# Emptying a PSUM bank with one relu copy, adding beta to x ahead, and scaling means on ScalarE, in a four-layer graph attention stack

## The chip, the cores and the metric

The kernel runs on one core of a Trainium2 chip. The metric is the device time of one execution in microseconds. The engines are TensorE (PE in the profile; its weight loads are PEld), VectorE (DVE), ScalarE (ACT), GpSimd (POOL) and SyncE (SP), which only issues DMAs. Each engine works through its own queue in order; semaphores order the engines among themselves.

## The reference

There are 16 graphs of 1024 nodes with 256 features, and four layers. Each layer adds to `x` what an attention over the graph's edges makes of the normalised, relu'd `x`. The third layer is the one that the change touches most:

```
h = maximum(layernorm(x), 0)                       # every layer, over the 256 features
v = h @ W                                          # layers 0 to 2: four heads of 64; layer 3: one of 256
e = leaky_relu(s_src[i] + s_dst[j]); e = -inf where adj[i, j] == 0
out = softmax(e over j) @ v
x = x + out                                        # layers 0, 1 and 3
# layer 2, the third one, per head:
o = relu(softmax(e) @ v + bias) + v
x = x + (o - mean(o)) / sqrt(var(o) + 1e-6) * gamma + beta
```

## The kernel before

**What is on the chip.** Nodes are tiled by 128: a graph has 8 blocks (`NB`). `x_cur` holds a graph's `x` in SBUF through all layers (128 x 8 x 256, float32); it is changed in place. A *unit* is one layer of one graph. For a head `h` of a unit, the numerators of the softmax are made transposed, block `j` of the sources against all 1024 targets: `cover` is one VectorE instruction (`SCALAR_TENSOR_TENSOR p<-r,fac,mask`, 128x1024) that writes one of 12 tiles `p`. Its operand `r` is a PSUM tile with a row spread over the partitions, which ScalarE copies there (`COPY r<-rows`).

**Groups and banks.** `gather` multiplies a tile `p` by the 64 columns of `v` and a column of ones. Eight tiles (`j` = 0 to 7) add up in one PSUM bank, called `po`: one bank for one half (`i`, four blocks of 128 targets) of one head, of 4 x 65 columns. This is a *group*. There are two `po` banks, so a group can only begin when the group before the last has left its bank. All matrix products are in float32. In the third layer the columns come from `v_flat`, a copy of `v` with the bias added.

**Emptying a bank.** `evacuate` (line 1312) does it. In the first two layers ScalarE copies the whole bank to the SBUF tile `att` (`COPY att<-po`, 128x260), and the division by the sums is done later in `finish`. In the third layer VectorE first takes the reciprocal of the four sums in the bank (line 1325), and then ScalarE takes each of the four blocks through a relu with the reciprocal as its scale, from the bank to `att` (lines 1327 and 1328). The bank is free when the last of the four is done. There are 16 x 4 x 2 = 128 such evacuations. There are three `att` tiles (`ATTS`); one is in use from the first evacuation of a head to the end of its `finish`.

**Finishing a head.** In the third layer `finish` (line 1341) adds `v` to `att` (128x512), VectorE makes statistics (`bn_stats`, eight of 128x64), GpSimd merges them (`merged`, with a power for the inverse root), ScalarE normalises with eight instructions (`ACTIVATE att<-att,s`), and then come three 128x512 instructions: times gamma, plus beta (line 1384), and the add to `x_cur` (line 1385). `either` gives these to GpSimd, or to VectorE at the very end of the kernel. When all heads of a unit are finished, the next layer of that graph may be prepared.

**Preparing a unit.** `prepare` (line 949) makes the statistics of `x_cur`, normalises (`hn`), transposes on TensorE, takes the relu on ScalarE (`hT<-pp`) and projects (`pp<-wa,hT`), and ScalarE copies the result to `v` (`v<-pp`, `v_one<-pp` for the last layer). Two banks, `pp`, serve these and the last layer's sums. For the first layer of the graphs from the third on (`ACT_STATS`, `BY_ACT`), 14 units, ScalarE makes the statistics: eight sums, then GpSimd scales them by -1/256 (line 974), then eight sums of squares about that mean.

**Order.** The order on every engine is made while the program is built. `Plan` keeps a clock for each engine and a table of costs; the loop at line 1589 always takes the step that can begin first, among jobs written as generators (`yield engine, ready`). An engine wrapped by `plan.engine` books its cost with each instruction; `nc.scalar`, `nc.vector` and `nc.gpsimd` issue without booking, and `plan.spend` books without issuing. The order of three graphs in different layers is interleaved (`ORDER`), so that the last layer's sums, the projections and the groups of several graphs share TensorE. The wrapper is the reason why nearly every line of the profile carries line 515.

Of the kernel before, what the change touches and what calls it, by code (L numbers as in the profile page):

```python
# [16 lines left out]
AF = mybir.ActivationFunctionType  # L17
ALU = mybir.AluOpType
# [518 lines left out]
def fast_path(  # L537
# [21 lines left out]
    nc = tc.nc  # L559
    ctx.enter_context(tc.manual_schedule())  # L560
    plan = Plan()
    pe, act, dve, pool, sp = (
        plan.engine(e, name)
        for e, name in (
            (nc.tensor, "PE"),
            (nc.scalar, "ACT"),
            (nc.vector, "DVE"),
            (nc.gpsimd, "POOL"),
            (nc.sync, "SP"),
        )  # L570
    )
    G, N, F = x.shape
# [3 lines left out]
    QUAD = 4  # L576
# [31 lines left out]
    bias_r, gamma_r, beta_r = (const.tile([P, F], F32, name=n) for n in ("bias_r", "gamma_r", "beta_r"))  # L608
# [46 lines left out]
    def bank():  # L655
        k = min(free_banks(), key=lambda k: banks[k])
        banks[k] = None
        if k >= BANKS:
            spare[0] += 1
            return ps_o.tile([P, 512], F32, name="po"), k  # L660
        return ps_p.tile([P, 512], F32, name=f"pp{k}"), k
# [20 lines left out]
    def wide_bank(dt=F32):  # L682
        k = wide_free.index(min(t for t in wide_free if t is not None))
        wide_free[k] = None
        return ps_r.tile([P, 4096 // mybir.dt.size(dt)], dt, name=f"r{k}"), k
# [249 lines left out]
    def merged(st: bass.AP, rs: bass.AP, w: int, eps: float, eng=pool):  # L935

        m0, m1, q0, q1 = st[:, :, 0, 1], st[:, :, 1, 1], st[:, :, 0, 2], st[:, :, 1, 2]
        shift, spread, inv = (rs[:, i, :] for i in range(3))
        eng.tensor_tensor(inv, m0, m1, ALU.subtract)
        eng.tensor_tensor(spread, q0, q1, ALU.add)  # L940
        eng.tensor_tensor(inv, inv, inv, ALU.mult)
        eng.tensor_tensor(shift, m0, m1, ALU.add)
        eng.tensor_scalar(inv, inv, 0.25, eps, ALU.mult, ALU.add)
        eng.tensor_scalar(spread, spread, 1.0 / w, 0.0, ALU.mult, ALU.add)
        eng.tensor_tensor(spread, spread, inv, ALU.add)
        pool.tensor_tensor(inv, spread, neg_half, ALU.pow)
        eng.tensor_scalar(shift, shift, -0.5, 0.0, ALU.mult, ALU.add)

    def prepare(u: "Unit"):

        n, w, layer = u.n, u.w, u.layer
# [16 lines left out]
        st = small.tile([P, NB, 2, 3], F32, name="st", bufs=2)  # L968
        rs = small.tile([P, 3, NB], F32, name="rs", bufs=4)
        if by_act:  # L970
            for i in range(2 * NB):
                if i == NB:
                    yield "POOL", None
                    pool.tensor_scalar(rs[:, 0, :], st[:, :, 0, 0], -1.0 / F, 0.0, ALU.mult, ALU.add)
                if i:
                    yield "ACT", None
                seen = work.tile([P, N], FP8, name="seen", bufs=1)[:, : 2 * F].bitcast(BF16)
                b, c = i % NB, i // NB
                if c:
                    act.activation(  # L980
                        seen, xt[:, b, :], AF.Square, bias=rs[:, 0, b : b + 1], accum_out=st[:, b, 1, 0:1]
                    )
                else:
                    act.activation(seen, xt[:, b, :], AF.Identity, accum_out=st[:, b, 0, 0:1])
            yield "POOL", None
            pool.tensor_scalar(rs[:, 1, :], st[:, :, 1, 0], 1.0 / F, 1e-5, ALU.mult, ALU.add)
            pool.tensor_tensor(rs[:, 2, :], rs[:, 1, :], neg_half, ALU.pow)
        else:
            for i in range(NB):
                if i:  # L990
                    yield "DVE", None
                dve.bn_stats(st[:, i].rearrange("p c s -> p (c s)"), xt[:, i, :])
            eng, name = (dve, "DVE") if u is main[0] else either()
            yield name, None
            merged(st, rs, F, 1e-5, eng)
            u.g.centred = plan.now
# [26 lines left out]
        if u is main[0]:  # L1023
            keep_warm(WARM_MAX)
        yield "PE", free_bank
        pm, k = bank()
# [10 lines left out]
            scale=top,  # L1037
# [4 lines left out]
        pa, k = bank()  # L1042
# [9 lines left out]
        eng, name = (dve, "DVE") if u is main[0] else either()  # L1052
# [29 lines left out]
        if direct:  # L1082
# [5 lines left out]
            for h in range(DIRECT_HEADS if n > 1 else 1):  # L1088
                pr, k = wide_bank()
# [22 lines left out]
        pr, k = bank()  # L1112
        turned(pr, mine[:, 0, :])
        yield "DVE", None, AT_ONCE
        row = small.tile([P, P // 2], F32, name="row", bufs=1)
# [196 lines left out]
    def evacuate(u: "Unit", i: int, h: int, po, turn: int):  # L1312

        w = u.w
        q = slice(i * QUAD, (i + 1) * QUAD)
        yield "ACT" if u.shared else "DVE", lambda: finishing[0] < ATTS or (u, h) in taking
        if (u, h) not in taking:
            finishing[0] += 1
            taking[u, h] = [work.tile([P, NB, w + 1], F32, name="att", bufs=ATTS), 0]
        att = taking[u, h][0]  # L1320
        if u.shared:
            act.copy(att[:, q, :], po)
        else:
            inv = u.inv[:, h, q]
            dve.reciprocal(inv, po[:, :, w])
            yield "ACT", None
            for k in range(QUAD):
                act.activation(att[:, i * QUAD + k, :w], po[:, k, :w], AF.Relu, scale=inv[:, k : k + 1])
        opened[turn] = plan.now
        taking[u, h][1] += 1  # L1330
        if taking[u, h][1] == 2:

            by = -(10**6) if u.layer < 2 or at_tile[0] > len(tiles) - LAST else at_tile[0] + LATER
            add(by, finish(u, h, att[:, :, :w], att[:, :, w]), plan.now)

    def either():

        idle = at_tile[0] == len(tiles) and plan.free["DVE"] <= plan.free["POOL"] + SOONER
        return (dve, "DVE") if idle else (pool, "POOL")

    def finish(u: "Unit", h: int, att, total):

        n, w = u.n, u.w
        at = h * (w + 2)
        wide = lambda ap: ap.unsqueeze(2).to_broadcast([P, NB, w])
        row = lambda ap: ap[:, h * w : (h + 1) * w].unsqueeze(1).to_broadcast([P, NB, w])
        xs = u.g.x[:, :, h * w : (h + 1) * w]

        eng, name = either()
        if u.shared:  # L1350
            yield "DVE", None
            dve.reciprocal(u.inv[:, h, :], total)
            eng, name = either()
            yield name, None
            eng.tensor_mul(att, att, wide(u.inv[:, h, :]))
        else:
            yield name, None
        if u.layer == 2:
            eng.tensor_add(att, att, u.v[:, :, at : at + w])
            u.added += 1  # L1360
            u.v_done = u.added == n
            yield "DVE", None
            s = small.tile([P, 4, NB], F32, name="s", bufs=ATTS)
            st = small.tile([P, NB, 2, 3], F32, name="st64", bufs=ATTS)
            for b in range(NB):
                dve.bn_stats(st[:, b].rearrange("p c s -> p (c s)"), att[:, b, :])
            eng, name = either()
            yield name, None
            merged(st, s, w, 1e-6, eng)
            if name == "DVE":  # L1370
                yield "DVE", None
                eng.tensor_add(att, att, wide(s[:, 0, :]))
                eng.tensor_mul(att, att, wide(s[:, 2, :]))
            else:
                pool.tensor_mul(s[:, 1, :], s[:, 0, :], s[:, 2, :])
                for b in range(NB):
                    yield "ACT", None
                    act.activation(
                        att[:, b, :], att[:, b, :], AF.Identity, bias=s[:, 1, b : b + 1], scale=s[:, 2, b : b + 1]
                    )  # L1380
                eng, name = either()
                yield name, None
            eng.tensor_mul(att, att, row(gamma_r))
            eng.tensor_add(att, att, row(beta_r))
        eng.tensor_add(xs, att, xs)
        finishing[0] -= 1
        u.finished[h] = plan.now
        if len(u.finished) == n:
            u.spent = True
            yield "DVE", None  # L1390
            at = u.g.b * LAYERS + u.layer
            inv = u.inv.rearrange("p h b -> p (h b)")
            dve.tensor_reduce(greatest[:, at : at + 1], inv, AX.X, ALU.add)
            summed.append(plan.now)
# [189 lines left out]
    def add(until, gen, ready, first=None):  # L1584
        jobs.append([until, ready, *(first or next(gen))[:2], gen])
# [103 lines left out]
```

## Time and profile before

| | |
|---|---|
| median of 3 runs | 2668.16 us (2663.21 to 2668.47) |
| profiled execution | 2667.53 us, span of its instructions 2665.8 us |
| granted TensorE clock | 0.997 |
| TensorE busy | 2578.2 us, 97% |
| VectorE busy | 2342.0 us, 88% |
| GpSimd busy | 1890.4 us, 71% |
| ScalarE busy | 1272.3 us, 48% |
| DMA | 69 GB/s on average, 184.44 MB |

In a line of a group, `out<-in` are the program's tiles with buffer numbers left out, then the shapes, the number of instructions, the busy time in us and the mean duration in ns, and behind the bar the idle time of the engine before them and what ended it. In a timeline, a line begins with the start in us and the busy time in us; lines that follow each other on one engine are merged; in square brackets stands the idle time before and what ended it. In the waits, "A <- B: total, times, longest" is time for which A's engine was idle until B was done. "issue" is a wait for nothing that the profile shows. The busy time of a matmul is modelled from its start, so that TensorE can be shown as busy for some tens of ns in which it waits.

### The profile page before, as it was taken

The page shows a single profiled execution, that of the slowest core. Times are in us where ns is not written, and L with a number is a line of the kernel's source. Part 1 is how long each engine was busy: PE and PEld are TensorE (multiplying, and loading weights), DVE is VectorE, ACT ScalarE, POOL GpSimd, SP SyncE. Part 2 cuts the span into 40 slices and gives each one's busy share as a digit, 9 for nine tenths or more (in the row PEclk, how much of TensorE's full clock was granted, in tenths as well). Part 3 has the DMA queues.
Part 4 walks back from the last instruction along what each step waited for, and adds up shares of the span by engine and source line. Part 5 has one row for each costly group of instructions (what it writes and reads, how often), then busy time and mean ns, then how long its engine had stood idle before and what let it go on. Part 6 is the DMA issues. An engine that isn't in the chain of part 4 may idle for free. (4 is left out here: it accounts for less than half of the span.)

```text
span 2665.8 us, 132436 instructions
## 1 busy us (share of the span) xinstructions
PE 2578.2 (97%) x59354; PEld 2207.9 (83%) x59354; DVE 2342.0 (88%) x3723; ACT 1272.3 (48%) x3378; POOL 1890.4 (71%) x3375
## 2 busy tenths in 40 slices
PE   9999999999999999999999999999999999899998
PEld 7888887787988788889888788988778798888775
DVE  6799998897999797889998897999888699998984
ACT  4633563654346456533564644356364553443441
POOL 5556888765778877747887875688787565977761
PEclk9999999999999999999999999999999999999999
DMA  8533233443132253313314441323334441111100
GB/s 133 84 75 73 59 69 69 76 87 71 64 66 63 63 85 82 76 57 77 72 55 82 88 72 59 83 50 75 74 74 79 83 85 57 53 47 55 40 23 32
DMA packets 211122, 184.44 MB, mean 69 GB/s; under 512 B 150640, under 2 KB 184560, under 8 KB 210544
## 3 DMA queue, kind: packets, MB, share of 16 engines
q1 hardware_dynamic: 143088, 159.10, 20.7%
q0 software_dynamic: 67456, 16.78, 10.3%
q8 instruction: 467, 7.65, 1.2%
q14 instruction: 111, 0.91, 0.1%
HBM read 191.77 MB, written 34.39 MB: 85 GB/s over the span
## 5 line engine op out<-in xcount | busy, mean ns | idle before, releaser
L515 DVE SCALAR_TENSOR_TENSOR p<-r,fac,mask 128x1024 f32<-128x1024 f32 (+2 forms) x2032 | 2075.7, 1079 | 159.8 <-PE pp L515 80.8
L515 PE MATMUL po<-v,p 128*64 128x65 f32 x32992 | 1060.9, 224 | 36.4 <-issue 15.8
L515 PEld LDWEIGHTS po<-v,p 128*64 128x64 f32 x32992 | 1021.5, 138 | 87.9 <-issue 30.8
L515 PEld LDWEIGHTS po<-v_flat,p 128*64 128x64 f32 x16384 | 507.8, 138 | 56.8 <-issue 24.4
L515 PE MATMUL po<-v_flat,p 128*64 128x65 f32 x16384 | 525.0, 223 | 29.4 <-issue 14.7
L515 PE MATMUL pp<-wa,hT 128*64 128x264 f32 (+1 forms) x4032 | 474.2, 385 | 0.1
L515 PE MATMUL pp<-v_one,p 128*64 128x257 f32 x3584 | 403.6, 380 | 3.2 <-ACT y L515 2.9
L515 PEld LDWEIGHTS pp<-wa,hT 128*64 128x64 f32 x4032 | 278.4, 137 | 132.1 <-ACT v L515 0.4
L515 PEld LDWEIGHTS pp<-v_one,p 128*64 128x64 f32 x3584 | 248.6, 136 | 128.0 <-ACT y L515 4.6
L515 POOL TENSOR_SCALAR hn<-x_cur,rs 128x256 f32<-128x256 f32 x504 | 274.6, 558 | 33.3 <-PE pp L515 29.3
L515 POOL TENSOR_TENSOR att<-att,inv 128x512 f32<-128x512 f32 x128 | 133.7, 1045 | 221.2 <-DVE inv L515 207.7
L515 ACT COPY att<-po 128x260 f32<-128x260 f32 x256 | 96.2, 376 | 377.1 <-PE po L515 353.1
L515 ACT COPY v<-pp 128x264 f32<-128x264 f32 (+1 forms) x392 | 148.5, 379 | 215.0 <-PE pp L515 213.8
L515 POOL TENSOR_TENSOR x_cur<-att,x_cur 128x512 f32<-128x512 f32 x190 | 225.8, 1188 | 14.9
L515 ACT COPY r<-rows 128x1024 f32<-128x1024 f32 x190 | 194.0, 1021 | 21.8 <-DVE p L515 15.5
L515 ACT ACTIVATE att<-att,s 128x64 f32<-128x64 f32 x512 | 190.9, 439 | 23.3 <-POOL s L515 23.0
L515 ACT ACTIVATE hT<-pp 128x512 f32<-128x512 f32 x250 | 136.4, 598 | 128.1 <-PE pp L515 127.4
L515 ACT ACTIVATE att<-po,inv 128x64 f32<-128x64 f32 x512 | 118.7, 321 | 145.6 <-DVE inv L515 143.6
L515 POOL TENSOR_TENSOR y<-y,x_cur 128x256 f32<-128x256 f32 x116 | 84.3, 732 | 131.6 <-ACT y L515 112.1
L515 POOL TENSOR_TENSOR v<-v,fac 128x512 f32<-128x512 f32 x131 | 136.2, 1064 | 11.5 <-ACT fac L515 11.4
L515 DVE BATCH_NORM_STATS2 st<-x_cur 128x6 f32<-128x256 f32 x400 | 138.3, 411 | 3.3 <-DMA x_cur<-in_x_dram 2.9
L515 PE MATMUL pp<-ident,hn 128*128 128x128 f32 x1000 | 137.0, 280 | 0.2 <-DVE row L515 0.2
(124 smaller groups left out, 2150.0 us busy)
## 6 DMA issues: line engine op xcount, KB each, us to landing
rows<-line SPq DMA_DIRECT2D x190, 512.0 KB
out_dram<-y SPq DMA_DIRECT2D x128, 128.0 KB
x_cur<-in_x_dram SPq DMA_DIRECT2D x112, 128.0 KB
near<-in_adj_dram POOLq DMA_DIRECT2D x112, 128.0 KB, 4.3
rows_one<-line SPq DMA_DIRECT2D x13, 512.0 KB
x_cur<-in_x_dram SPq DMA_DIRECT2D x4, 512.0 KB
line<-row SPq DMA_DIRECT2D x96, 8.0 KB
block<-in_adj_dram POOLq DMA_DIRECT2D x4, 256.0 KB, 10.4
```

The lines of the kernel that those rows point to most:

```text
L515: r = call(*a, **k)
```

## The change

In `evacuate`, for the third layer: ScalarE copies the whole bank through a relu to `att`, VectorE takes the reciprocals of the sums from `att`, and ScalarE multiplies the four blocks in `att`, in place. In `finish`, for the third layer: beta is added to `x_cur` right behind the add of `v` to `att`, on the same engine; the add of beta to `att` is gone. In `prepare`: the 128x8 means are scaled by ScalarE. The new instructions are issued without booking, and what they replace is booked where it was.

```
@@ prepare @@
                 if i == NB:
                     yield "POOL", None
-                    pool.tensor_scalar(rs[:, 0, :], st[:, :, 0, 0], -1.0 / F, 0.0, ALU.mult, ALU.add)
+                    nc.scalar.activation(rs[:, 0, :], st[:, :, 0, 0], AF.Copy, scale=-1.0 / F)
+                    plan.spend(
+                        "POOL", *plan.cost("POOL", "tensor_scalar", (rs[:, 0, :],), {}), [st.tensor.name], [rs.tensor.name]
+                    )
@@ evacuate @@
             inv = u.inv[:, h, q]
-            dve.reciprocal(inv, po[:, :, w])
+            nc.scalar.activation(att[:, q, :], po, AF.Relu)
+            nc.vector.reciprocal(inv, att[:, q, w])
+            plan.spend("DVE", *plan.cost("DVE", "reciprocal", (inv,), {}))
             yield "ACT", None
             for k in range(QUAD):
-                act.activation(att[:, i * QUAD + k, :w], po[:, k, :w], AF.Relu, scale=inv[:, k : k + 1])
+                one, of = att[:, i * QUAD + k, :w], inv[:, k : k + 1]
+                nc.scalar.activation(one, one, AF.Copy, scale=of)
+                plan.spend("ACT", *plan.cost("ACT", "activation", (one, of), {}), [], [att.tensor.name])
@@ finish @@
             eng.tensor_add(att, att, u.v[:, :, at : at + w])
+            {"DVE": nc.vector, "POOL": nc.gpsimd}[name].tensor_add(xs, xs, row(beta_r))
...
             eng.tensor_mul(att, att, row(gamma_r))
-            eng.tensor_add(att, att, row(beta_r))
+            plan.spend(name, *plan.cost(name, "tensor_add", (att,), {}), [att.tensor.name], [att.tensor.name])
         eng.tensor_add(xs, att, xs)
```

## Prediction

> **What bounds the kernel now.** I read the page first, then who waits for whom on TensorE, then the busy time of each engine in stretches of the span.
>
> ```profile
> span 2665.8 us, 132436 instructions
> PE 2578.2 (97%) x59354; PEld 2207.9 (83%) x59354; DVE 2342.0 (88%) x3723; ACT 1272.3 (48%) x3378; POOL 1890.4 (71%) x3375
> ```
>
> TensorE is the bound over the whole span: it is idle for 2665.8 - 2578.2 = 87.6 us, and no change to the other engines can give back more. The waits split that idle time:
>
> ```profile
> PE po L515 <- ACT att L515: 15.8, 16, 1.4
> PE po L515 <- DVE p L515: 9.4, 9, 2.7
> ```
>
> The first line is what the relu copy aims at: a group's PSUM bank (`po`) was not yet emptied. I followed each of these waits in the timeline: 13, of 11.5 us in all, stand before the first matmul of a group whose bank a third-layer group held; the longest (1.36 us) recurs at 783.6, 1271.6 and 1756.9 us, so the schedule repeats every 488 us or so. Where do they lie? Stretches of the windows view, one in each repetition (columns: stretch, its length, busy PE, PEld, DVE, ACT, POOL):
>
> ```profile
> 264.00:342.00 78.00, 73.03 (x2136) 67.74 (x2132) 77.75 (x118) 42.01 (x127) 68.06 (x115) 1.00 0.29 60
> 752.00:830.00 78.00, 72.69 (x2115) 67.29 (x2112) 76.89 (x117) 41.38 (x126) 66.68 (x113) 1.00 0.29 59
> 1240.00:1318.00 78.00, 73.13 (x2136) 67.77 (x2134) 77.94 (x118) 41.76 (x128) 67.42 (x113) 1.00 0.30 60
> 1725.00:1803.00 78.00, 73.39 (x2149) 68.06 (x2145) 78.00 (x118) 41.89 (x127) 67.25 (x114) 1.00 0.30 60
> 2255.00:2340.00 85.00, 77.39 (x2183) 72.64 (x2180) 84.60 (x137) 34.07 (x99) 73.98 (x137) 0.96 0.15 49
> ```
>
> Here VectorE is busy 395.2 of 397 us: it, not TensorE, sets the pace. TensorE is idle 27.4 us here, and the timeline shows it taking tile after tile 0.05 us after VectorE made it. Twelve of the 13 bank waits lie in these five stretches; the thirteenth is 0.26 us. Outside them TensorE is the bound and VectorE is some 2 to 8 us of tiles ahead.
>
> **Prices.** From the groups, shapes kept apart:
>
> ```profile
> L515 ACT ACTIVATE att<-po,inv 128x64 f32<-128x64 f32 x512 | 118.7, 321 | 145.6 <-DVE inv L515 143.6 <-DVE wide L515 0.8
> L515 ACT COPY att<-po 128x260 f32<-128x260 f32 x256 | 96.2, 376 | 377.1 <-PE po L515 353.1 <-POOL hn L515 11.3 <-POOL x_cur L515 9.9
> L515 DVE RECIPROCAL inv<-po 128x4 f32<-128x4 f32 x128 | 22.5, 176 | 21.4 <-PE po L515 20.3
> L515 POOL TENSOR_TENSOR att<-att,beta_r 128x512 f32<-128x512 f32 x62 | 73.6, 1187 | 4.9
> ```
>
> The built programs, set side by side, have the same order on TensorE and SyncE; on the others only the changed instructions differ. So every gain or loss is a wait that gets shorter or longer.
>
> **The relu copy.** It adds 128 instructions at 0.376 us (the first two layers' copy of the same 128x260) to ScalarE: 48 us on an engine that is idle half the time, which by itself costs nothing. Three effects matter.
>
> (a) The bank. Before, it was free a reciprocal and four scalings after the group's end: 1.2 to 2.2 us. After, 0.05 + 0.38 = 0.43 us if ScalarE is free. But 11.3 of the 11.5 us lie where VectorE is saturated: TensorE gets its bank earlier and then waits as much longer for the next tile. I take -0.3 us. The bounds are 0 and -11.5.
>
> (b) The reciprocal. It is in VectorE's queue, with the covers (`p`) behind it, and waited for TensorE; now it waits for ScalarE's copy, which ends 0.47 us after the group's end at the earliest. Where VectorE arrived sooner it now stands still. Example, ScalarE's and VectorE's timelines around the group that ended at 294.77:
>
> ```profile
> 294.69 0.93 ACT L515 ACTIVATE att<-po,inv 128x64 f32<-128x64 f32 x4 [0.78 <-DVE inv L515]
> 295.49 1.04 ACT L515 COPY r<-rows 128x1024 f32<-128x1024 f32 x1
> 296.43 0.95 ACT L515 ACTIVATE att<-po,inv 128x64 f32<-128x64 f32 x4
> ...
> 295.74 0.17 DVE L515 RECIPROCAL inv<-po 128x4 f32<-128x4 f32 x1
> ```
>
> In the new order this group's relu stands on ScalarE where the second four scalings stood, behind the first four and the `r` copy: it ends at 296.43 + 0.45 = 296.9, and the reciprocal of 295.74 is 1.2 us late. In the first stretch VectorE loses 0.2 (271.7) + 0.4 (280.3) + 1.2 (295.7), less the 0.25 for which it waited anyway at 308.25: 1.55. In the second 0.4 (758.4) + 0.4 (768.2) + 1.1 (783.7, the same pattern) less 0.15: 1.75; the third the same; the fourth without the first 0.4: 1.4; the fifth 0.4 + 0.5 + 0.4 less 0.15: 1.15. VectorE has no idle time to absorb it there, so the kernel is later by the sum: 7.6 us. Bounds: 2 (one wait of 0.4 in each stretch) and 11 (every wait in them). Outside these stretches VectorE loses some 40 us in the same way, covered by its tiles ahead; with that cover gone it would all count.
>
> (c) What stands behind on ScalarE. Relu, then a trip to VectorE, then the scalings, and ScalarE's next copies wait. ScalarE's timeline from 358 (between the lines shown stand four scalings at 358.86, two `hT` copies at 359.64 and an `r` copy at 360.60):
>
> ```profile
> 357.80 1.06 ACT L515 ACTIVATE seen<-mask 128x1024 fp8e4<-128x1024 fp8e4 x1
> ...
> 361.54 0.97 ACT L515 ACTIVATE att<-po,inv 128x64 f32<-128x64 f32 x4
> 362.33 0.82 ACT L515 COPY v_one<-pp 128x258 f32<-128x258 f32 x2
> ```
>
> Each of the two evacuations grows by about 0.35 (relu) + 0.3 (ScalarE idle during the reciprocal of 0.18 and two signals). The `v_one` copy is then 1.3 us late; TensorE refills its bank at 363.02, 0.3 us after it was free, so TensorE stalls about 1.0 us. This recurs at 846, 1334 and 1819: 4.0 us. Lesser cases of the same kind (505, 992, 1479 and 1965 us: 0.3 each; 2355: 0.3) make 1.5. Around 2510 a late reciprocal and `r` copy delay a tile that TensorE took 0.05 us after it was made: 0.5. Together 6.0; bounds 0 (ScalarE's queue closes up) and 9.
>
> The scalings now read SBUF. The nearest rows are copies scaled by a pointer from SBUF, 299 ns for 128x4 and 309 for 128x16: at that slope 64 elements take 349 ns, against 321 from PSUM. That is 0.03 us each, inside the bounds of (c).
>
> The Trainium skill (Perfetto Trace Analysis, Optimizing Scalar/DVE Operations) speaks against this edit: ScalarE pays about 93 ns of access on SBUF and 51 on PSUM. By it the 512 scalings would cost ScalarE 21 us instead of the 14 that my slope makes. The same page (Optimization Strategy) says that the same gap repeating on the engine that should be saturated can mean too little PSUM for the next tile, which would credit (a) with its full 11.5 us. The stretches above say that another engine is saturated just there.
>
> **Beta ahead.** The number of adds stays. The one behind gamma goes: a head's end comes 1.25 us sooner on GpSimd. The new add follows `att + v` on the same engine, where GpSimd often waits for the statistics (2.3 us at 396). It pays where somebody waits for `x_cur` (the beta add stands just before the first line, at 408.31):
>
> ```profile
> 409.58 1.18 POOL L515 TENSOR_TENSOR x_cur<-att,x_cur 128x512 f32<-128x512 f32 x1
> 410.80 0.38 ACT L515 COPY att<-po 128x260 f32<-128x260 f32 x1 [2.48 <-POOL x_cur L515]
> ```
>
> That copy waits for an `att` buffer, and TensorE is idle 1.25 us for its bank (411.2; also 900.2, 1387.4, 1872.4). The chain gains 1.25 and loses 0.4 to the late reciprocal at 395.7: -0.85 x 4 = -3.4. At the end, VectorE's beta add of 1.25 us at 2597.8 lies on the chain to the last graph's first transpose, before which TensorE is idle 1.83 us: -1.25 + 0.4 = -0.85. Sum -4.3; bounds -6.5 and 0.
>
> **Means by ScalarE.** Fourteen tiny instructions leave GpSimd (204 ns each), with a trip of about 1 us at 330.2, 818.1, 1305.9 and 1791.2. No one on TensorE or VectorE waits for it: 0, bounds -1 and +1.
>
> **Sum.** -0.3 + 7.6 + 6.0 - 4.3 = +9.0 us on the profiled execution's 2667.5 us (span 2665.8 and 1.7 around it): 2676.5. The median of the runs, 2668.2, is 0.6 us above that execution.
>
> **Rivals.**
> - *Faster: the banks pay.* If VectorE's saturation is only apparent, because the earlier bank also brings reciprocals forward, (a) gives up to -11.5 and (b) vanishes: -11.5 - 4.3 + 3 (half of c) = -13, 2655 us. For it: the gaps recur and end in `ACT att`. Against: VectorE's 1.8 us of idle time in 397. It decides once (b) is under 2 us.
> - *No difference.* ScalarE is idle half the time; if its queue closes up, (c) is 0 and (b) only 4: +4 - 4.3 = 0, about 2668. For it: leads of 2 to 8 us outside the stretches. Against: the chained evacuations at 295 and 358.
> - *Much slower.* The 101 reciprocals that VectorE reaches before the copy is done lose 51 us in all; if half of it reached TensorE, 2690.
>
> **How the numbers follow.** Forecast 0.55, faster rival 0.17, no difference 0.22, much slower 0.06. What a measurement here can tell from no change is about 0.2%, 5.3 us, the width of the three runs. Range 2657 to 2690: it takes in the forecast with the bounds of (b) and (c), no difference, and the edge of the faster case; the forecast's own range is 2671 to 2686. Chances: faster 0.17, same 0.22, slower 0.61.
>
> **What would show it.** Right: waits of `PE po` for `ACT att` fall from 15.8 to under 6 us, while waits for `DVE p` grow by more; a new line "DVE inv <- ACT att" of some tens of us; `v_one` copies near 365 followed by a TensorE gap of about 1 us; no gap at 411. Wrong: TensorE's idle time falls below 80 us, or VectorE is idle in the five stretches without the stretches getting longer.

## The result and the profile after

The changed kernel is slower.

| | before | after |
|---|---|---|
| median of 5 runs | 2668.47 us (2663.21 to 2671.81) | 2690.5 us (2683.56 to 2694.84) |
| ratio | | 1.008, 95% interval 1.0061 to 1.01: +16 to +27 us |
| profiled execution | 2667.53 us, span 2665.8 | 2694.84 us, span 2692.9 |
| TensorE busy / idle | 2578.2 / 87.6 us | 2594.9 / 98.0 us |

The profiled execution of after is the slowest of its five: 4.2 of its 27.1 us arise in the first 160 us, before any third-layer bank is emptied. Sizes below therefore come from the ratios of the timed runs (ratio less one, times the median of before in the same call); profiles are used for places and causes.

The head of the page of after:

```profile
span 2692.9 us, 132602 instructions
PE 2594.9 (96%) x59354; PEld 2215.4 (82%) x59354; DVE 2344.2 (87%) x3722; ACT 1331.0 (49%) x3520; POOL 1887.3 (70%) x3362
```

ScalarE has 58.7 us more to do and is still idle half the time. The waits, TensorE's first, then VectorE's new one:

```profile
PE po L515 <- DVE p L515: 16.7, 15, 2.7
PE pp L515 <- ACT hT L515: 8.8, 10, 1.4
PE pp L515 <- ACT v_one L515: 3.4, 4, 0.8
...
PE po L515 <- ACT att L1334: 1.1, 1, 1.1
PE po L515 <- ACT att L1328: 0.8, 1, 0.8
...
DVE inv L1329 <- ACT att L1328: 52.8, 78, 3.2
```

The waits at which the relu copy aimed are nearly gone: 1.9 us are left of the 11.5 for third-layer banks. In their place `DVE p` grew from 9.4 to 16.7 us, and there are waits that before did not have. The groups of TensorE's projections show these best; the last part of a line is the idle time before them. First before, then after:

```profile
L515 PE MATMUL pp<-wa,hT 128*64 128x264 f32 x3040 | 358.4, 386 | 0.1
L515 PE MATMUL pp<-wa,hT 128*64 128x258 f32 x992 | 115.8, 380 | 0.0
```

```profile
L515 PE MATMUL pp<-wa,hT 128*64 128x264 f32 x3040 | 360.4, 387 | 12.8 <-ACT hT L515 8.6 <-ACT v L515 2.0 <-DVE c L515 1.9
L515 PE MATMUL pp<-wa,hT 128*64 128x258 f32 x992 | 116.3, 381 | 3.8 <-ACT v_one L515 3.4
L515 PE MATMUL pp<-ident,wide 128*64 128x64 f32 x496 | 36.8, 225 | 2.7 <-ACT wide L515 2.0 <-ACT hT L515 0.2 <-DVE wide L515 0.2
```

TensorE used to enter its projections with no wait; now it stands 16.6 us before them, and 2.7 (0.4 before) at `wide`. Most of these waits are for copies by ScalarE that stand behind an evacuation. Four waits of 0.7 us for `hT` (565.8, 1061.5, 1551.7 and 2041.0 us) are not: with beta alone they are there too (0.42 to 0.44 us), with the relu copy alone they are not. Waits for `hT` and `wide` of 6.9 us in all lie in the five stretches below.

The five stretches in which VectorE was saturated, between the same matmuls as before (columns: stretch, length, busy PE, PEld, DVE, ACT, POOL, clock, DMA):

```profile
268.01:348.86 80.85, 74.41 (x2137) 68.28 (x2133) 78.22 (x118) 45.39 (x137) 69.42 (x115) 1.00 0.28 58
761.83:845.47 83.64, 75.34 (x2117) 69.39 (x2113) 77.84 (x117) 45.03 (x135) 69.04 (x114) 0.98 0.28 56
1256.92:1337.02 80.10, 74.01 (x2134) 68.18 (x2132) 78.09 (x117) 45.34 (x137) 68.56 (x113) 1.00 0.29 58
1746.27:1826.50 80.23, 74.97 (x2148) 68.88 (x2145) 78.56 (x118) 45.57 (x137) 68.70 (x114) 1.00 0.29 58
2279.92:2367.56 87.64, 78.25 (x2182) 72.92 (x2180) 84.70 (x136) 37.73 (x107) 73.94 (x137) 0.96 0.14 47
sum 412.46, PE 376.98 PEld 347.65 DVE 397.40 ACT 219.06 POOL 349.65; mean PE 75.40 PEld 69.53 DVE 79.48 ACT 43.81 POOL 69.93
```

Their sum went from 397.3 us, between these matmuls, to 412.5, +15.1. VectorE does the same work in them (395.5 and 397.4) and is now idle 15.1 us instead of 1.8; added over the gaps in these stretches, 13.4 of the 15.1 stand before a reciprocal that waits for the relu copy. So the earlier banks bought nothing here: VectorE paces these stretches, and VectorE was slowed.

### The profile page after: what moved, and what is told of

Read it like the earlier page. It is cut to its first block, busy times and chain, and to the rows that moved or that the text cites. A ratio compares the mean times of both kernels' runs of the same rounds, so it can differ in the third digit from the quotient of the medians.

```text
span 2692.9 us, 132602 instructions
## 1 busy us (share of the span) xinstructions
PE 2594.9 (96%) x59354; PEld 2215.4 (82%) x59354; DVE 2344.2 (87%) x3722; ACT 1331.0 (49%) x3520; POOL 1887.3 (70%) x3362
## 5 line engine op out<-in xcount | busy, mean ns | idle before, releaser
L515 PE MATMUL po<-v,p 128*64 128x65 f32 x32992 | 1065.7, 225 | 34.3 <-issue 17.8
L515 PE MATMUL pp<-wa,hT 128*64 128x264 f32 (+1 forms) x4032 | 476.7, 386 | 16.7 <-ACT hT L515 8.6
L515 POOL TENSOR_TENSOR x_cur<-att,x_cur 128x512 f32<-128x512 f32 x190 | 225.5, 1187 | 14.9
L1334 ACT ACTIVATE att<-att,inv 128x64 f32<-128x64 f32 x512 | 135.7, 338 | 31.6 <-DVE inv L1329 31.5
L515 POOL TENSOR_TENSOR v<-v,fac 128x512 f32<-128x512 f32 x131 | 136.0, 1061 | 12.2 <-ACT fac L515 12.2
```

Of the source, the lines that this page charges most:

```text
L515: r = call(*a, **k)
L1334: nc.scalar.activation(one, one, AF.Copy, scale=of)
```

## The experiments

All ratios are against before in the same call, with the 95% interval, and in us by that call's median of before. Theory at the outset: the relu copy with its trip ScalarE, VectorE, ScalarE makes the whole loss; beta ahead gains a little; means do nothing.

**The three parts alone.** Each takes one of the three edits of the change, as the diff above has it.

> Only the relu copy with the reciprocal and the scalings behind it; beta and means as before. Theory (the round trip: the reciprocal waits for ScalarE's copy, the scalings wait for the reciprocal, and ScalarE's next copies wait behind them): all of the loss and the 4.3 us that beta was said to gain on top, +20 to +30 us against before; TensorE waits for `ACT hT` and `ACT v_one`, and the 1.25 us gaps near 411 us stay. Rival (GpSimd's order, by beta or the means, makes the loss): within 5 us of before.

> Only beta, added to x ahead. Theory: -4 us (-7 to 0): the four gaps near 411, 900, 1387 and 1872 us and 0.9 us at the end. Rival (beta makes part of the loss, because the add ahead delays GpSimd's merging of the statistics): slower by 5 us or more.

> Only the means scaled by ScalarE. Both theories that put the loss at the third layer's banks: 0, within 3 us of before. Rival (the instruction waits on ScalarE for the accumulated sums, and copies wait behind it): slower by 5 us or more.

| part | ratio | us |
|---|---|---|
| relu copy alone | 1.0106 (1.009 to 1.0123) | +28 (+24 to +33) |
| beta ahead alone | 0.9988 (0.9979 to 0.9996) | -3.2 (-5.6 to -1.1) |
| means alone | 0.9993 (0.9983 to 1.0003) | -1.9 (-4.5 to +0.8), not told from zero |

The parts add up to +23, the whole is +21. The relu copy is the loss, and more than the whole of it. Its profiled execution is the median of its five, so its profile has the loss at its usual size: 27.8 us longer than that of before, of which 15.4 in the five stretches. VectorE is idle 15.3 us there, 14.4 of them before a reciprocal that waits for the copy. The other 12.4 us arise outside.

**Is it ScalarE's load?** Before each third-layer evacuation ScalarE does one more relu of 128x256 in SBUF, which nobody needs:

```
+            aside = work.tile([P, N], FP8, name="seen", bufs=1)[:, : 2 * F].bitcast(BF16)
+            nc.scalar.activation(aside, gamma_r, AF.Relu)
             dve.reciprocal(inv, po[:, :, w])
```

> The kernel before, with one extra relu of 128x256 on ScalarE (SBUF to SBUF, about 0.4 us) just ahead of each of the 128 reciprocals' places, which nobody needs and which waits for nothing; bank, reciprocal and scalings as before. Theory (round trip and waiting): +0 to +5 us. Rival (ScalarE's extra 48 us of work is enough to make the copies of hT and v late): +12 us or more.

Measured 1.0012 (1.0002 to 1.0022): +3 us (0.5 to 6). Load alone is no explanation. But this load stands where ScalarE often waits for the reciprocal anyway (143.6 us of such waits before), so it says nothing of work that stands behind that wait; a later run had to.

**The trip without the long copy.** ScalarE copies only the four sums, the reciprocal reads them there, the scalings read the bank as before:

```
-            dve.reciprocal(inv, po[:, :, w])
+            nc.scalar.copy(att[:, q, w], po[:, :, w])
+            nc.vector.reciprocal(inv, att[:, q, w])
```

> ScalarE copies only the four sums (128x4) out of the bank; VectorE takes the reciprocal of that copy; the four scalings read the bank as before. So the trip ScalarE, VectorE, ScalarE is as in the change, but the copy is short (some 0.25 us by the nearest rows, against 0.38), no scaling reads SBUF and the bank is freed late. Theory (the trip in the order of the queues costs the time): slower by 15 to 30 us, with VectorE's reciprocals again waiting some 50 us in all for ScalarE and new TensorE waits for hT, v_one and wide; since the bank is freed later than before, waits of po for att grow too. Rival (the long copy and the scalings from SBUF cost it): at most +8 us.

Measured 1.0063 (1.0049 to 1.0076): +17 us (13 to 20). So the trip costs about that much, with a copy of only 168 ns, and VectorE's wait is there:

```profile
DVE inv L1326 <- ACT att L1325: 34.2, 63, 1.9
```

The loss is half of these 34 us, but not all of it need be VectorE's: as expected, the bank came later, and TensorE's waits of `po` for `att` rose from 15.8 to 19.3 us. The new TensorE waits for `hT` and `wide` that were expected did not appear, though: the projections of 264 columns wait 0.8 us here, against 12.8 in after. So they need more than the trip.

**The scalings on GpSimd.** ScalarE's four scalings are left out, and GpSimd multiplies the whole tile in `finish`:

```
+            nc.scalar.activation(att[:, q, :], po, AF.Relu)
+            nc.vector.reciprocal(inv, att[:, q, w])
...
+            own.tensor_mul(att, att, wide(u.inv[:, h, :]))
             eng.tensor_add(att, att, u.v[:, :, at : at + w])
```

> One relu copy empties the bank, and the reciprocal follows it at once on VectorE, as in the change; the four scalings on ScalarE are left out, and GpSimd multiplies the whole tile by the reciprocals once, ahead of the add of v (64 multiplies of about 1.04 us). So the reciprocal still waits for ScalarE, but nothing on ScalarE waits for the reciprocal. Theory: the loss by hT, v_one and wide (some 20 us of the relu copy alone's 28) goes, the loss by the late reciprocal (DVE p, some 7 us) stays: +2 to +10 us against before, plus what 67 us more on GpSimd may cost at tiles that wait for x_cur. Rival (VectorE's late reciprocal is what makes everything late): +20 us or more.

Measured 1.0052 (1.0037 to 1.0066): +14 us (10 to 18), half of the relu part's 28. TensorE's waits for `hT` and `v_one` are gone from its list, those for `DVE p` stay (17.8 us). As expected in direction; the 67 us on GpSimd are in it, and the run with no multiply below prices them.

**The same with the reciprocal late.** One reciprocal of eight sums in `finish`, just ahead of that multiply, instead of two at the evacuations:

```
-            nc.vector.reciprocal(inv, att[:, q, w])
...
+            nc.vector.reciprocal(u.inv[:, h, :], total)
             own.tensor_mul(att, att, wide(u.inv[:, h, :]))
```

> As the kernel with the scalings on GpSimd, but also the reciprocal moves: one of eight sums for each head, ahead of GpSimd's multiply, as in the first two layers. Nothing on VectorE or ScalarE waits for the other within the evacuation, and the bank is freed by one copy. Theory (the trip is the loss, the bank itself is worth little where VectorE is saturated): between -8 and +2 us against before; it should be 5 us or more faster than the kernel with the early reciprocal. Rival (an early bank is worth its 11 us of gaps): -11 us or better. Rival (GpSimd's 67 us count): +5 or more.

A clear miss: 1.0228 (1.0214 to 1.0241), +61 us. The trace says why; VectorE's longest list of waits is new:

```profile
DVE st L515 <- POOL att L515: 78.2, 61, 3.3
```

The edit took one trip away and made a worse one: the reciprocal now stands on VectorE shortly ahead of the statistics of the same tile, and between the two GpSimd has a multiply and an add to do, some 2.2 us. VectorE stands still for it. The granted clock was lower too, 0.990 against 0.997. The run can't say what an early bank is worth, but it is one more case of the same cause: an instruction that waits for another engine, in an order made for a world where it didn't.

**The reciprocal reads the bank beside the copy.** The relu part with this one edit:

```
             nc.scalar.activation(att[:, q, :], po, AF.Relu)
-            nc.vector.reciprocal(inv, att[:, q, w])
+            nc.vector.reciprocal(inv, po[:, :, w])
```

> The whole relu part of the change, with one edit: VectorE's reciprocal reads the four sums from the bank, as in the kernel before, beside ScalarE's relu copy, and no longer that copy. The scalings still read the copy in SBUF on ScalarE. So VectorE waits for TensorE alone, and ScalarE's chain is the longer of copy and reciprocal, then the scalings. Theory (VectorE's wait for ScalarE is the heart of the loss, and what is late on ScalarE is mostly its consequence): +2 to +10 us against before, 15 or more less than the relu part as it is. Rival (the copy itself, standing ahead of hT, v_one and r in ScalarE's order and waiting there for the group's end, makes the loss): +15 to +28 us, as with the relu part.

Measured 1.0093 (1.0079 to 1.0107): +25 us (21 to 29). Taken at its word this would sink the theory. But the wait was not gone. VectorE's timeline:

```profile
296.24 0.18 DVE L1326 RECIPROCAL inv<-po 128x4 f32<-128x4 f32 x1 [0.53 <-ACT att L1325]
...
298.77 0.18 DVE L1326 RECIPROCAL inv<-po 128x4 f32<-128x4 f32 x1 [1.18 <-ACT att L1325]
```

The reciprocal reads `po` and yet waits for ScalarE's copy (48.3 us in 77 waits, against 52.8 in after): the built program orders the second reader of a bank behind the first. The run shows only that the source of the reciprocal is of little account, and that its place in the program matters.

**The two runs beside it.** With the reciprocal written as in that kernel, the multiply once on GpSimd, and once left out, so that the division by the sums is missing:

> The reciprocal reads the bank as before; one relu copy empties it; the scalings are one multiply of the whole tile on GpSimd ahead of the add of v (64 of 1.05 us), none on ScalarE. No engine waits inside the evacuation for another one than TensorE. Against the kernel with the same multiply on GpSimd and the reciprocal of the copy (+14 us) this takes away only VectorE's wait. Theory: 10 to 18 us less than that kernel, so -5 to +4 against before. Rival (GpSimd's 67 us make the loss there): no more than 4 us less than that kernel.

> As the kernel with the reciprocal from the bank and the multiply on GpSimd, but without the multiply: the division by the sums is left out. ScalarE has 256 short scalings fewer in 128 evacuations, VectorE and GpSimd are as before, the bank is free after one copy. It bounds what the early bank can bring. Theory (where VectorE is saturated the bank is worth little): -6 to 0 us. Rival (the 11.5 us of gaps are all to be had): -10 us or better. Against the kernel with the multiply it shows what GpSimd's 67 us cost.

With the multiply 1.007 (1.0055 to 1.0085), +19 us (15 to 23); without it 1.0035 (1.0022 to 1.0048), +9 us (6 to 13). VectorE waits for the copy in both (38.0 and 36.9 us), so neither does what its expectation says. They give two prices. GpSimd's 67 us cost some 9 us (19 less 9, with both intervals around it), though GpSimd is 71% busy. And the bank freed by one copy, with VectorE's late reciprocal but with all 512 scalings (118.7 us) off ScalarE, still loses 9 us: the early bank does not even pay for the late reciprocal. In the five stretches VectorE is idle 6.5 us in this kernel, 6.3 of them before its reciprocals, and they last 401.3 us instead of 397.3.

**The reciprocal first.** To take the trip away, the program's order has to be turned round:

```
             dve.reciprocal(inv, po[:, :, w])
+            nc.scalar.activation(att[:, q, :], po, AF.Relu)
             yield "ACT", None
...
-                act.activation(att[:, i * QUAD + k, :w], po[:, k, :w], AF.Relu, scale=inv[:, k : k + 1])
+                nc.scalar.activation(one, one, AF.Copy, scale=of)
```

> The relu part again, with the reciprocal issued ahead of the relu copy. In the kernel that let both read the bank, the reciprocal stood behind the copy in the program and still waited for it (48 us in 77 waits), so that kernel did not take the wait away. Here the reciprocal reads the bank as in the kernel before and waits for TensorE alone; ScalarE waits for it once, as before, and then does copy and scalings (from SBUF) in one piece. ScalarE's work is as in the relu part: 0.38 us for the copy and 4 x 0.017 for the scalings more at each of 128 evacuations. Left out is only the second trip: VectorE's wait for ScalarE, and ScalarE's for VectorE between copy and scalings. Theory (the trip makes the loss): waits of VectorE's reciprocal for ScalarE gone, +2 to +10 us against before, of which an added load on ScalarE alone measured 3 to 5; some 18 or more less than the relu part's +28. Rival (0.45 us more on ScalarE ahead of hT, v_one, wide and r makes the loss): +18 us or more.

Measured 1.0054 (1.0036 to 1.0072): +14 us (10 to 19), between what theory and rival expected. VectorE's reciprocal waits for TensorE again, and the scalings (L1330) wait for nobody:

```profile
DVE inv L515 <- PE po L515: 25.2, 28, 3.0
```

```profile
L1330 ACT ACTIVATE att<-att,inv 128x64 f32<-128x64 f32 x512 | 135.6, 338 | 2.8
L1326 ACT ACTIVATE att<-po 128x260 f32<-128x260 f32 x128 | 48.7, 382 | 133.5 <-DVE inv L515 131.7 <-DVE wide L515 0.8
```

The copy now waits for the reciprocal, of which it needs nothing. And TensorE's projections still wait, 10.2 us where it was 16.6 in after:

```profile
L515 PE MATMUL pp<-wa,hT 128*64 128x264 f32 x3040 | 359.3, 387 | 6.9 <-ACT hT L515 5.7 <-ACT v L515 1.1
L515 PE MATMUL pp<-wa,hT 128*64 128x258 f32 x992 | 116.6, 381 | 3.3 <-ACT v_one L515 2.5 <-issue 0.8
```

Those waits are not where most of the time goes, though. The profiled execution is 9.8 us longer than that of before, and the five stretches alone are 10.4 us longer. VectorE is idle 10.4 us in them: 3.7 before reciprocals that wait for TensorE (2.3 of it right behind a TensorE gap to "issue"), 1.1 before those that wait for ScalarE's copies of the first two layers, 1.7 before `wide` for ScalarE's `v`, and 3.5 in a wait that before did not have, of the statistics for the `att` to which GpSimd adds `v` behind the scalings:

```profile
DVE st L515 <- POOL att L515: 9.4, 17, 1.0
```

So the theory held for half and has to be split. The trip costs about 14 us (28 less 14; the kernel with the trip and the short copy gave 17). The other 14 are left for the longer piece on ScalarE, which is all that this edit adds to its work: behind the reciprocal stand 0.38 us of copy and four scalings that keep ScalarE busy 33 ns longer each, ahead of GpSimd's add of `v` and of `hT`, `v` and `v_one`. That is a remainder, not a run of its own. 17 and 14 are 31; the relu part is 28 (24 to 33). The load run may have missed this half because its copy stood ahead of the wait.

**What beats both.** Beta and means, with the evacuation of before:

> The two other parts of the change together, with the evacuation as before. Alone they measured -2.7 and -1.6 (not told from zero) us. Expected: -3 to -5 us against before.

Measured 0.9987 (0.9978 to 0.9997): -3.5 us (-0.8 to -5.9), faster than before and some 25 us faster than after.

## Why the prediction was right, and where its sum fell short

The direction and its reasons held; the change costs 16 to 27 us where the sum had +9. The measured 2690 us lies at the upper edge of the stated range and above the forecast's own 2671 to 2686: that the range reaches so far is owed to its width, not to the sum. Both terms of loss were too small by half. For the relu copy the sum had 7.3 us in the five stretches, (a) and (b), and 6.0 outside, (c); the relu part alone lost 15.4 and 12.4.

- **(a) The bank, -0.3.** The judgement held, on the place where it was made. The gaps for third-layer banks fell from 11.5 to 1.9 us, and the stretches that held twelve of the thirteen grew by 15.1 us. (The timeline has 12 such gaps that end with `ACT att`, 10.8 us; the thirteenth, 0.8 us at 2271.7, ends with `DVE st`.) One sign failed: waits for `DVE p` grew by 7.3 us, less than the 13.9 by which the waits for `ACT att` fell. The Trainium skill's rule of the repeating gap (Perfetto Trace Analysis, Optimization Strategy), which would have credited 11.5 us, did not apply here: the gap repeated, the banks came earlier, and the kernel without any scalings was still 9 us slower than before. The rule says "can mean", and the windows view told that VectorE was saturated just there.
- **(b) The late reciprocal, +7.6, with bounds 2 and 11.** The mechanism held, the size was too small. VectorE's waits for the copy in the stretches are 13.4 us; less the 1.2 us for which the reciprocals waited before, 12.2, above the upper bound (13.2 in the relu part alone). The longest, 3.15 us at 780.96, stands behind 2.3 us that TensorE had lost to "issue". Without these 2.3 it would be 9.9, but they are no accident of one execution: the relu part alone has 2.3 us of "issue" before the same matmul, the kernel before has none there, and why is not shown. The example came out to a tenth: predicted 1.2 us late, and in after VectorE's and ScalarE's timelines there read

```profile
301.99 0.18 DVE L1329 RECIPROCAL inv<-att 128x4 f32<-128x4 f32 x1 [1.18 <-ACT att L1328]
```

```profile
301.59 0.37 ACT L1328 ACTIVATE att<-po 128x260 f32<-128x260 f32 x1
302.20 1.07 ACT L1334 ACTIVATE att<-att,inv 128x64 f32<-128x64 f32 x4 [0.25 <-DVE inv L1329]
303.18 1.09 ACT L515 ACTIVATE att<-att,s 128x64 f32<-128x64 f32 x3
304.17 1.05 ACT L515 ACTIVATE hT<-pp 128x512 f32<-128x512 f32 x2
```

  Where I expected "the same pattern" with 1.1 us in the next three stretches it is 0.65; part of what the sum lacks are waits of 0.3 to 0.4 us that I had not listed (809.04 and 811.94, and the same again in the next two stretches).

  Outside the stretches I counted VectorE's lateness at nothing. Its total was right (51 forecast, 52.8 measured). Whether some of it counts outside too is open: the kernel with the short copy lost 17 us of its 34, but its profile, which is of its fastest run, has +9, of which 7.0 in the stretches.
- **(c) ScalarE's next copies, +6.0 with bounds 0 and 9.** Too small as well, though the places were mostly right: the four gaps for `v_one` are 0.84 us where I wrote 1.0, those for `v` near 505 and its repeats 0.5 where I wrote 0.3, and four of 0.5 for VectorE's `c` came on top. Outside the stretches TensorE's waits for `hT`, `v_one`, `v`, `wide` and `c` make 8.2 us in the relu part alone, of 12.4 us lost there; what the rest is stays open. The relu part less the kernel without scalings is 28 - 9 = 19 us, but that is not (c) alone: without scalings VectorE waits 6.3 us before its reciprocals in the stretches, with them 14.4, so some 8 of the 19 are rather (b)'s, whose example has the relu copy standing behind another bank's scalings. What I did not see stands in the lines just shown: two `hT` copies behind the same evacuation. I followed this piece of ScalarE for what it does to the reciprocal and not for what stands behind it. TensorE's timeline:

```profile
304.80 1.56 PE L515 MATMUL pp<-wa,hT 128*64 128x264 f32 x12 [1.06 <-ACT hT L515]
```

  It repeats at 801.08 (1.43), 1293.38 (1.42) and 1782.9 us (1.43), 5.3 us in all. These four lie in the stretches that VectorE paces, where nearly all of VectorE's idle time stands before the reciprocals. They show how late ScalarE is; that they cost anything of their own is not shown.
- **Scalings from SBUF, 349 ns.** One takes 338, against 321 from PSUM: 17 ns. But neighbours overlap, so ScalarE's time is the busy time of the 512, and that rose from 118.7 to 135.7 us: 17 us, or 33 ns each, where my slope made 28 ns and 14 us. The Trainium skill's access figures (Perfetto Trace Analysis, Optimizing Scalar/DVE Operations: about 93 and 51 ns of the engine's time) give an estimate of 42 ns and 21 us; the measured rows lie between the two. "Inside the bounds of (c)" and "by itself costs nothing" were too easy: with the copy this is the longer piece on ScalarE, to which the kernel with the reciprocal first leaves half of the loss.
- **Beta ahead, -4.3.** Measured -3.2 alone (-5.6 to -1.1). The gap at 411 us, which I had named, is gone: TensorE goes through from 418.42 to 420.53. The four waits of 0.4 us for `hT` that beta brings were not in the sum.
- **Means, 0.** Measured as not told from zero.
- **The rivals.** "Faster" and "no difference" failed on their own conditions: (b) was not under 2 us, and ScalarE's queue did not close up. "Much slower", given 0.06 and 2690 us, has the right time, but that is in part luck: it took half of VectorE's lateness and nothing from ScalarE's late copies. In after 13.4 of the 52.8 us lie in the stretches, and what the rest costs is open.

TensorE's busy time rose by 16.7 us with the same 59354 matmuls. A part can be waiting that the model of matmul ends counts as busy, a part the lower granted clock of this execution (0.995 against 0.997; an estimate from these two is 5 us). They were not separated, so the gaps of TensorE name the causes but do not add up to the loss. The clock does not make the loss: beside the relu part alone, before's runs at 0.995 took 2669.8 to 2671.6 us, and the relu part's, at 0.995 to 0.998, 2694.5 to 2700.4.

## What to carry to other kernels

When a step that reads a result directly is split into "copy, then another engine, then back", price it in two places: on the engine that now waits in its queue, and on every instruction that stands behind the returning work, the ones other engines need most of all. Count each wait where it lies: the waits of an engine that does not set the pace there can be long and free. An engine that is idle half the time can still be on the path at the moment when its next copy is due. And a gap that repeats can be worth nothing if another engine is saturated in just that stretch: look at the windows before crediting it.

## What the runs showed of the hardware and its program

- Two engines that read the same bank were not free of each other: in this program the reader written second waits for the one written first, the reciprocal for the copy (48.3 us in 77 waits) or, with the reciprocal first, the copy for the reciprocal (131.7 us in 69 waits). Neither needs the other's result.
- One GpSimd add of 128x512 took 1278 ns as `x_cur` plus beta, against 1187 for `att` plus beta; I have no explanation.
- One kernel has a lower granted clock than the others: 0.990 to 0.995 over the five runs with the late reciprocal. All others, before too, lie between 0.995 and 0.999. What is cause there and what is effect was not tried.
